# Attention and involution on one core: the last image's first convolution made directly, new cost constants, smaller last blocks, last units in parts

## The chip, the cores and the metric

The kernel runs on one core of a Trainium2 chip. The metric is the device time of one execution in microseconds (us). The core has five engines that run side by side and wait for each other by semaphores: TensorE (PE in the profile; its weight loads are PEld), VectorE (DVE), ScalarE (ACT), GpSimd (POOL) and SyncE (SP, which here only issues DMAs). All data is fp32. An fp32 matmul shows as two TensorE instructions in the trace.

## The reference

Input x has 4 images of 512 channels and 64 x 64 pixels (n = 4096). Two layers follow each other:

```
q, k, v = wq x + bq, wk x + bk, wv x + bv        # 512 -> 128 channels
x = wo (v softmax(q^T k)^T) + bo + x              # attention over the 4096 pixels
o = relu(s1 * (W1 x) + b1)                        # first convolution, 512 -> 128
w = Ws relu(sr * (Wr o) + br) + bs                # 8 groups x 49 taps for each pixel
y[c, p] = sum over 49 taps of w[group(c), tap, p] * o[c, p shifted by tap]
out = s3 * (W3 y) + b3 + x                        # 128 -> 512
```

The 7 x 7 neighbourhood is padded with zeros by 3 on each side. A group has 16 channels.

## The kernel before

**Chunks and images.** An image is cut into 8 chunks of 512 pixels (8 image rows). For each image, `keys_values` makes keys and values for all chunks (weights `wk`, `wv`), then `attention` goes through the chunks' queries. A step of attention is one 128 x 512 tile of scores: `pss` (TensorE), `pt` = exponential (ScalarE), `po` += values (TensorE), and `pacc` += `pt` on VectorE, which gathers the softmax denominators. A chunk has 32 steps. In the last image the last chunk is done as two blocks of 256 queries with 16 steps each. Scores are made two steps ahead. The `pss` and `pt` tiles have 2 and 5 buffers.

**Finishing a block** (`finish_block`, L520): `on` is copied from `po`, the denominators are summed (`sums`, `blocks`, `pl`), inverted (`rls`) and spread (`spread`), and `on` is multiplied by them. Four matmuls `pwo` with the output weights follow; L560 adds each to x, with the bias `bo`. The first convolution `p1` (four matmuls over the new x) and its Relu `o1` (L573) come next. In the last image `o1` is transposed by TensorE (`pp`) and written to a padded image in DRAM (`pix`). `pr` and `red` make the 32 reduced channels that the tap weights come from, and `last_bias` adds the last bias to x.

**Units.** The involution works in units of 4 image rows (two tiles of 2 rows, 128 pixels each; 16 units an image). Rows come back from `pix` into a ring of 12 rows, where entry r holds the 7 shifted copies of rows r and r+1. `pump` (L240) issues those loads as rows are written and ring space is free (`low`, `load`). For a unit, `weights` makes the tap weights `pw`. Then VectorE multiplies ring rows by weights (`prod`, or `acc` for the first, L356): for each of 7 column shifts once 4 row shifts (128 x 1024 elements) and once 3 (128 x 768). Where the ring wraps, a group is split in two. GpSimd adds each product to `acc` (L380). After attention of the last image has ended (`tail` is set), every second product is added by TensorE, as matmuls with the identity into `pa` (L375). At the end the parts of `acc` are folded (L389; in the tail by TensorE into `pa`), turned to channels first (`accT`), multiplied by W3 (`py`) and added to x (L461). Then the chunk, or in the last chunk the half, is stored.

**What sets the order.** The order is written by a planner while the program is built. Attention's steps run in a fixed loop. After each, `chores` (L269) takes one step of finishing, one of closing, and as many taps as `pace` allows. `pe` is the planner's TensorE clock; `free["dve"]` and `free["pool"]` are times at which it thinks that VectorE and GpSimd will have done what they were given, kept by the constants of L68 to L70. A tap is issued only if

```
pe >= max(begin, landed)
free["dve"] <= pe + 3.5          # 4.5 in the last image
free["pool"] <= pe + lag         # 4.0 during keys and values, 7.5 in attention
```

and if the budget `due` (1.56 tap rows a microsecond, at most 20) is at least 2. In the last image `pause` and `until` hold a finishing block until the planner thinks that VectorE is done with the step before. In the tail none of this holds: finishing, closing and taps take turns. Products have 4 buffers, tap weights 1 (2 in the tail), `red` has 3, and the general PSUM pool (`mm`) 2.

The kernel also holds a general path that runs only if a check of the denominators fails; it plays no part here.

Of the kernel before, what the change touches and what calls it, by code (L numbers as in the profile page):

```python
# [15 lines left out]
P = 128  # L16
# [42 lines left out]
SR = UR + K - 2  # L59

DYS = (0, 4), (4, 3)
TAPS_A_US = 1.56

PE_COLUMN = 0.43 / 256
DVE_OP, POOL_OP = 0.7, 1.28  # L68
DVE_TAPS, POOL_TAPS = (0.16, 0.27), (0.19, 0.55)
ROW_US, X_US, PIX_US, LAND_US = 2.2, 3.8, 1.5, 3.0  # L70
HOP_US = 0.8
STEP_US = 1.0
# [11 lines left out]
def fast_path(  # L84
# [91 lines left out]
    def takes(engine, us):  # L176
        free[engine] = max(free[engine], pe) + us
        return free[engine]
# [61 lines left out]
    def pump():  # L240

        nonlocal load
        while load // STEP in written:
            b, row = divmod(load, STEP)
            rows, us = written[b]

            end = H + SR - UR if rows == H else rows + PAD - 1
            n = min(b * STEP + end, low + RING) - load
            n = min(n, RING - load % RING, PIECE if b == B - 1 else RING)
            if n <= 0:  # L250
                break
# [20 lines left out]
        pace()  # L272


    def weights(b, u):
        red, col = reds[b, u]
        wpools.append(wpools.pop(0))
        pw = wpools[0].tile([P, NT, CH], F32, tag="w", name=f"pw_{b}_{u}")
        for t in range(NT):

            rows = slice(t * (P // NT), t * (P // NT) + CR + 1)
            pixels = slice(col, col + P)
            mm(
                pw[:, t, : NTAP * G], red[rows, pixels], wt[rows, O_WT : O_WT + NTAP * G],
                shared=2,
            )
        return pw
# [15 lines left out]
        nc.vector.tensor_scalar(verdict, pn, P - 0.5, None, ALU.is_lt)  # L303


    def involution():
        nonlocal low, due
        while True:
            while not units:
                yield "none"  # L310
            b, u = units.pop(0)
            acc = work2.tile([P, NT, 4, P], F32, tag="acc", name=f"acc_{b}_{u}")
            yield from until(free["dve"] + 0.3)
            pw = early.pop((b, u), None) or weights(b, u)
# [9 lines left out]
            for o, (x, dy, n) in enumerate(ops):  # L324
                if o and dy >= DYS[1][0] > ops[o - 1][1]:
                    low = base + UR
                    pump()
                    if tail and units:
                        early[units[0]] = weights(*units[0])
                rows = [(base + dy + t * 2) % RING for t in range(NT)]  # L330
                while base + dy + n + NT > load:
                    yield "wait"
                landed = max(landing[base + dy + i] for i in range(n + NT))
                while not tail and (
                    pe < max(begin, landed)
                    or free["dve"] > pe + (4.5 if b == B - 1 else 3.5)
                    or free["pool"] > pe + lag
                ):
# [4 lines left out]
                d0 = dy - DYS[dy >= DYS[1][0]][0]  # L343
                first = x == 0 and dy < DYS[1][0]
                prod, p0 = acc, d0
                if not first:
                    prod, p0 = prods.tile(
                        [P, NT, 4, P], F32, tag="prod", name=f"prod_{b}_{u}_{o}"
                    ), 0
                col = (x * K + dy) * G  # L350
                lines = ring[:, rows[0] : rows[0] + n, x, :]
                image = bass.AP(
                    tensor=lines.tensor, offset=lines.offset,
                    ap=[lines.ap[0], [(rows[1] - rows[0]) * K * P, NT], [K * P, n], [1, P]],
                )
                product = nc.vector.tensor_tensor(  # L356
                    prod[:, :, p0 : p0 + n, :].rearrange("p t d (g c) -> p t d g c", g=G),
                    image.rearrange("p t d (g c) -> p t d g c", g=G),
                    pw[:, :, col : col + n * G].unsqueeze(3)
                    .broadcast_to([P, NT, n * G, GC])  # L360
                    .rearrange("p t (d g) c -> p t d g c", d=n),
                    ALU.mult,
                )
                if not tail:
                    tc.keep_in_program_order(product)
                if first:
                    pass
                elif tail and o % 2:

                    begun = pa is not None  # L370
                    if not begun:
                        pa = ps1.tile([P, NT, P], F32, tag=("po", "acc")[u % 2], name=f"pa_{b}_{u}")
                    for t in range(NT):
                        for d in range(n):
                            mm(  # L375
                                pa[:, t, :], prod[:, t, d, :], ident,
                                not begun and t == d == 0, False,
                            )
                else:
                    nc.gpsimd.tensor_tensor(  # L380
                        acc[:, :, d0 : d0 + n, :], acc[:, :, d0 : d0 + n, :], prod[:, :, :n, :],
                        ALU.add,
                    )
                yield
            low = max(low, (b + 1) * STEP if u == NU - 1 else base + UR)
            pump()
# [133 lines left out]
    def finish_block(b, c, off, n, po, sums):  # L520

        late = b == B - 1
        name = f"{b}_{c}_{off}"
        xt = xs[b, c][:, :, off : off + n]

# [29 lines left out]
        yield from pause(takes("dve", DVE_OP * n / CH), 5)  # L555
        for t in range(CT):
            pw = ps.tile([P, CH], F32, tag="mm", name=f"pwo_{name}_{t}")[:, :n]
            mm(pw, w_slice(O_WO, t), on)
            takes("dve", DVE_OP * n / CH)
            nc.vector.scalar_tensor_tensor(  # L560
                xt[:, t, :], pw, bo[:, t : t + 1], xt[:, t, :], ALU.add, ALU.add
            )
            for _ in range(t % 2 if late else 1 + (t != 1)):
                yield
        for _ in range(0 if late else 2):
            yield
        p1 = ps.tile([P, CH], F32, tag="mm", name=f"p1_{name}")[:, :n]
        for t in range(CT):
            mm(p1, w_slice(O_W1, t), xt[:, t, :], t == 0, t == CT - 1)
            if t == 1 and not late:  # L570
                yield
        o1 = work1.tile([P, CH], F32, tag="o1", name=f"o1_{name}")[:, :n]
        nc.scalar.activation(o1, p1, AF.Relu, bias=v1(V_B1), scale=v1(V_S1))  # L573

        def last_bias():

# [41 lines left out]
                    )  # L618
        us = takes("dma", PIX_US) + LAND_US

        pr = ps.tile([P, CH // NT], F32, tag="mm", name=f"pr_{name}")[:, : n // NT]
        for t in range(NT):
            half = slice(t * (P // NT), (t + 1) * (P // NT))
            mm(
                pr[half], w_slice(O_WP, 0)[:, half],
                o1.rearrange("p (u t x) -> p u t x", t=NT, x=P)[:, :, t, :], shared=2,
            )
        red = redpool.tile([P, CH // NT], F32, tag="red", name=f"red_{name}")[:, : n // NT]
        nc.scalar.activation(red, pr, AF.Relu, bias=v1(V_BP), scale=v1(V_SP))
        for i in range(tiles // NT):  # L630
            reds[b, top // UR + i] = red, i * P

        rows = top + n // W
        written[b] = rows, us
        units.extend((b, u) for u in range(top // UR, rows // UR))
        pump()
        yield
        if late:
            yield from last_bias()
        if (b, c) == (B - 1, NCH - 3):  # L640
# [65 lines left out]
    for b in range(B):  # L706
# [3 lines left out]
        if b == 0:  # L710
# [3 lines left out]
                tc.keep_in_program_order(mm(pb[:, t : t + 1], w_slice(O_WO, t), v1(V_BVC)))  # L714
            bo = const.tile([P, CT], F32, name="bo")
            nc.vector.tensor_tensor(bo, pb, vec[:, V_BO : V_BO + CT], ALU.add)
        attention(b, *kv)
    tail.append(True)
    scorepool.close()
# [405 lines left out]
```

## Time and profile before

| | us |
|---|---|
| median of 3 runs | 2606.61 |
| lowest, highest | 2604.79, 2607.39 |
| span of the profiled execution | 2605.7 |
| TensorE busy | 2587.9 (99%) |
| VectorE busy | 1874.2 (72%) |
| GpSimd busy | 1823.5 (70%) |
| ScalarE busy | 835.8 (32%) |

The profiled execution's own time is known by its span, from the first to the last instruction; it lies among the timed runs. A group's line gives source line, engine, operation, tiles, shape, count, then busy time and the mean of one. A window's line gives busy time and instruction count of each engine, TensorE's granted clock, and the share and rate of DMA. A piece of the chain is start, duration and what ran.

Units can be told apart in the trace by their first product, which writes `acc`. In the last image they start at 2070, 2103, 2150, 2189, 2223, 2262, 2295, 2333, 2368, 2408, 2439, 2478, 2514, 2542, 2556 and 2578 us. The blocks' reductions (`red`) are at 2047, 2115, 2192, 2265, 2336, 2408, 2477, 2516 and 2542 us, and the last `sums` of attention is at 2523.4.

### The profile page before, as it was taken

Reading aid. Unit: us, or ns where it says so; the run is one execution under the profiler, and the core shown is the slowest. Engines: PE = TensorE matmul, PEld = TensorE weight load, DVE = VectorE, ACT = ScalarE, POOL = GpSimd, SP = SyncE. Lnnn points to the kernel's source line nnn. Section 1 sums busy time; section 2 is a strip of 40 time slices with the busy share of each in tenths; the row PEclk is TensorE's granted clock in tenths of the full one; section 3 lists DMA queues with packets and bytes.
Section 4 is the critical chain, followed back from the end, with each engine's and each line's share of the span. In section 5 each row is a group of like instructions: output and inputs, shape, how many; then the busy total and the mean of one; then the engine's idle time right before and its main releaser. Section 6 shows DMA issues by size and latency. Waiting matters only on the chain.

```text
span 2605.7 us, 24569 instructions
## 1 busy us (share of the span) xinstructions
PE 2587.9 (99%) x7484; PEld 1246.5 (48%) x7484; DVE 1874.2 (72%) x2677; ACT 835.8 (32%) x1378; POOL 1823.5 (70%) x1197
## 2 busy tenths in 40 slices
PE   9999999999999999999999999999999999999998
PEld 7444444445544444444644444444464444444577
DVE  0447777877575787788676678788757678777887
ACT  1333333332233333333223333333323333333330
POOL 0007788877881788887885468888788577877886
PEclk9999999999999999999999999999999999999999
DMA  6033232445615344233651434443463433222343
GB/s 236 1 75 63 55 85 73 99 99 150 164 43 112 63 101 95 61 84 82 180 129 45 103 69 101 101 92 74 118 171 83 101 93 93 72 60 58 73 91 102
DMA packets 208798, 244.33 MB, mean 94 GB/s; under 512 B 109640, under 2 KB 128528, under 8 KB 208528
## 3 DMA queue, kind: packets, MB, share of 16 engines
q1 hardware_dynamic: 208224, 242.31, 38.6%
q8 instruction: 61, 1.00, 0.2%
q14 instruction: 81, 0.66, 0.1%
q10 hardware_dynamic: 432, 0.36, 0.0%
HBM read 193.57 MB, written 49.06 MB: 93 GB/s over the span
## 4 chain that ended last, share of the span: by engine, by line
PE 91%; POOL 4%; DVE 3%; issue 1%; DMA 0%; ACT 0%; SPq 0%; POOLq 0%; DVEq 0%; ACTq 0%
PE pss L220 32%; PE po L220 31%; PE pv L220 4%; PE pk L220 4%; PE pq L220 4%; PE pwo L220 4%; PE py L220 4%; PE p L220 4%; POOL acc L380 4%; PE pw L220 2%; DVE prod L356 1%; PE pa L220 1%; DVE pacc L696 1%; PE pr L220 1%; POOL acc L389 0%
## 5 line engine op out<-in xcount | busy, mean ns | idle before, releaser
L380 POOL TENSOR_TENSOR acc<-acc,prod 128x768 f32<-128x768 f32 (+3 forms) x1063 | 1701.5, 1620 | 760.5 <-DVE prod L356 712.4
L220 PE MATMUL pss<-q,k 128*128 128x512 f32 (+1 forms) x2112 | 1056.3, 585 | 0.0
L220 PE MATMUL po<-pt,v 128*128 128x512 f32 (+1 forms) x2112 | 1047.7, 581 | 0.0
L665 ACT ACTIVATE pt<-pss 128x512 f32<-128x512 f32 x1024 | 611.3, 597 | 1252.0 <-PE pss L220 1184.9
L356 DVE TENSOR_TENSOR prod<-ring,pw 128x512 f32<-128x512 f32 (+3 forms) x1092 | 886.7, 847 | 44.6 <-POOL acc L380 41.7
L696 DVE TENSOR_TENSOR pacc<-pacc,pt 128x512 f32<-128x512 f32 x958 | 664.6, 694 | 243.2 <-ACT pt L665 216.2
L220 PEld LDWEIGHTS po<-pt,v 128*128 128x128 f32 x2112 | 399.3, 190 | 482.2 <-issue 462.2
L220 PEld LDWEIGHTS pss<-q,k 128*128 128x128 f32 x2112 | 391.9, 190 | 466.2 <-issue 459.3
L404 DVE STREAM_TRANSPOSE turned<-acc 128x256 f32<-128x256 f32 x48 | 21.4, 446 | 217.4 <-POOL acc L389 217.4
L220 PE MATMUL py<-accT,wt 128*128 128x512 f32 (+1 forms) x264 | 132.3, 584 | 4.0 <-DVE x L461 3.3
L220 PE MATMUL pwo<-on,wt 128*128 128x512 f32 (+1 forms) x264 | 130.3, 586 | 0.0
L220 PEld LDWEIGHTS pv<-wt,x 128*128 128x128 f32 x1024 | 119.6, 192 | 15.3 <-issue 15.0
L389 POOL TENSOR_TENSOR acc<-acc 128x512 f32<-128x512 f32 x120 | 119.5, 996 | 9.4
L461 DVE SCALAR_TENSOR_TENSOR x<-py,vec,x 128x512 f32<-128x512 f32 (+1 forms) x132 | 95.7, 726 | 36.1 <-PE py L220 35.8
L220 PE MATMUL pv<-wt,x 128*128 128x128 f32 x1024 | 120.2, 275 | 0.0
L220 PE MATMUL p<-x,wt 128*128 128x512 f32 (+1 forms) x264 | 119.2, 579 | 0.0
L578 ACT ACTIVATE x<-x,vec 128x512 f32<-128x512 f32 (+1 forms) x132 | 92.9, 706 | 80.0 <-PE p L220 74.9
L220 PE MATMUL pk<-x,wt 128*128 128x512 f32 x256 | 117.3, 596 | 0.1
L220 PE MATMUL pq<-x,wt 128*128 128x512 f32 (+1 forms) x264 | 115.4, 580 | 0.0
L560 DVE SCALAR_TENSOR_TENSOR x<-pwo,bo,x 128x512 f32<-128x512 f32 (+1 forms) x132 | 95.2, 727 | 22.8 <-PE pwo L220 21.7
L356 DVE TENSOR_TENSOR acc<-ring,pw 128x1024 f32<-128x1024 f32 (+1 forms) x84 | 78.7, 955 | 17.6 <-PE pw L220 17.6
L220 PEld LDWEIGHTS pq<-x,wt 128*128 128x128 f32 x264 | 50.0, 190 | 60.2 <-issue 56.7
(57 smaller groups left out, 733.6 us busy)
## 6 DMA issues: line engine op xcount, KB each, us to landing
x<-x_dram SPq DMA_DIRECT2D x55, 1024.0 KB, 5.7
ring<-pix SPq DMA_DIRECT2D x74, 448.0 KB, 8.3
ring<-pix SPq DMA_DIRECT2D x24, 1344.0 KB, 9.7
out_dram<-x SPq DMA_DIRECT2D x31, 1024.0 KB, 4.2
ring<-pix SPq DMA_DIRECT2D x24, 896.0 KB, 10.7
ring<-pix SPq DMA_DIRECT2D x30, 672.0 KB, 10.2
ring<-pix SPq DMA_DIRECT2D x6, 2240.0 KB, 19.5
pix<-o1t SPq DMA_DIRECT2D x192, 32.0 KB, 1.7
```

What stands on the lines that cost most here:

```text
L220: return nc.tensor.matmul(o, lhsT=lhsT, rhs=rhs, start=start, stop=stop)
L356: product = nc.vector.tensor_tensor(prod[:, :, p0 : p0 + n, :].rearrange("p t d (g c) -> p t d g c", g=G), image.rearrange("p t d (g c) -> ...
L380: nc.gpsimd.tensor_tensor(acc[:, :, d0 : d0 + n, :], acc[:, :, d0 : d0 + n, :], prod[:, :, :n, :], ALU.add,)
L389: nc.gpsimd.tensor_tensor(acc[:, :, :n, :], acc[:, :, :n, :], acc[:, :, n : 2 * n, :], ALU.add)
L404: nc.vector.transpose(blocks.rearrange("p (t k q) -> p t k q", t=NT, q=TB), acc[:, :, 0, :].rearrange("p t (k q) -> p t k q", q=TB),)
L461: nc.vector.scalar_tensor_tensor(xt[:, t, :], py, v1(V_S3 + t), xt[:, t, :], ALU.mult, ALU.add)
L560: nc.vector.scalar_tensor_tensor(xt[:, t, :], pw, bo[:, t : t + 1], xt[:, t, :], ALU.add, ALU.add)
L578: nc.scalar.activation(xt[:, t, :], xt[:, t, :], AF.Identity, bias=v1(V_B3 + t))
L665: nc.scalar.activation(pt, pss, AF.Exp)
L696: nc.vector.tensor_tensor(paccs[k], paccs[k], pt, ALU.add)
```

## The change

Four things change together.

1. **Direct first convolution** for chunks 5 to 7 of the last image. Between keys and attention of the last image the product of output weights and first convolution is made (`w1wo`, with its bias `b1wo`). In these blocks `p1` is four matmuls over the old x plus one, `w1wo` on `on`. The residual (`pwo` and L560) comes after `o1` has been written and reduced.
2. **Constants** of the account: VectorE and GpSimd operations and taps are charged less.
3. **The last chunk's queries** in blocks of 256, 128 and 128. A block of 128 has one tile, so reductions are kept by tile (`reds`).
4. **Units 14 and 15 of the last image** are done in nine parts, given by tiles, first row shift and number of row shifts. Row shifts that meet only padding are left out, two ring rows are not loaded, and the part's number and column shift decide which engine adds.

The body of a tap becomes the function `multiply_add`.

```diff
+PADDED = 2
+LAST = (
+    (0, (0, 1), 0, 2), (0, (0, 1), 2, 2),
+    (0, (0, 1), 4, 2), (0, (0,), 6, 1), (1, (0,), 0, 4),
+    (0, (1,), 6, 1), (1, (1,), 0, 4), (1, (0, 1), 4, 1), (1, (0,), 5, 2),
+)
+DIRECT = 5
-DVE_OP, POOL_OP = 0.7, 1.28
-DVE_TAPS, POOL_TAPS = (0.16, 0.27), (0.19, 0.55)
+DVE_OP, POOL_OP = 0.62, 1.23
+DVE_TAPS, POOL_TAPS = (0.065, 0.267), (0.14, 0.545)
...
-            end = H + SR - UR if rows == H else rows + PAD - 1
+            end = H + SR - UR - PADDED * (b == B - 1) if rows == H else rows + PAD - 1
...
-    def weights(b, u):
-        red, col = reds[b, u]
-        wpools.append(wpools.pop(0))
-        pw = wpools[0].tile([P, NT, CH], F32, tag="w", name=f"pw_{b}_{u}")
-        for t in range(NT):
+    def weights(b, u, tiles=range(NT), pw=None):
+        if pw is None:
+            wpools.append(wpools.pop(0))
+            pw = wpools[0].tile([P, NT, CH], F32, tag="w", name=f"pw_{b}_{u}")
+        for t in tiles:
+            red, col = reds[b, u * NT + t]
...
+    def last_units(b, u0):
+        nonlocal low, due
+        accs, pas, pws, weighed = {}, {}, {}, set()
...
+        for i, (v, tiles, dy, n) in enumerate(LAST):
+            u = u0 + v
+            while v and not tail:
+                yield "wait"
+            base = b * STEP + u * UR
+            while base + dy + 2 * tiles[-1] + n > load:
+                yield "wait"
...
+            fresh = [t for t in tiles if (v, t) not in weighed]
+            if fresh:
+                pws[v] = weights(b, u, fresh, pws[v])
+                weighed.update((v, t) for t in fresh)
...
+            for x in range(K):
...
+                pas[v] = multiply_add(
+                    b, u, accs[v], pas[v], pws[v], tiles, x, dy, n, f"{i}_{x}",
+                    x == 0 and dy < DYS[1][0], bool(tail) and (x + i) % 2,
+                )
+                yield
+            if ends[v] == i:
+                closing.append(turn_unit(b, u, accs[v], pas[v], takes("pool", POOL_OP * 1.5)))
+        units.clear()
...
     def involution():
...
             b, u = units.pop(0)
+            if b == B - 1 and u == NU - 2:
+                yield from last_units(b, u)
+                return
...
     def finish_block(b, c, off, n, po, sums):
+        direct = late and c >= DIRECT
...
+        spreads = takes("dve", DVE_OP * n / CH)
+        def residual():
...
+        if not direct:
+            yield from pause(spreads, 5)
+            yield from residual()
...
+            mm(p1, w_slice(O_W1, t), xt[:, t, :], t == 0, t == CT - 1 and not direct)
+        if direct:
+            yield from pause(spreads, 0)
+            mm(p1, w1wo, on, False, True)
+        nc.scalar.activation(
+            o1, p1, AF.Relu, bias=b1wo if direct else v1(V_B1), scale=v1(V_S1)
+        )
...
+        if direct:
+            yield from residual()
         if late:
             yield from last_bias()
...
     def attention(b, kt, vT, q):
-            blocks[-1:] = [(NCH - 1, off, CH // 2) for off in (0, CH // 2)]
+            blocks[-1:] = [(NCH - 1, 0, 2 * P), (NCH - 1, 2 * P, P), (NCH - 1, 3 * P, P)]
...
+        if b == B - 1:
+            turned = work1.tile([P, CT, P], F32, tag="sums", name="wo_turned")
+            pt = ps.tile([P, CT, P], F32, tag="mm", name="pwot")
+            for t in range(CT):
+                nc.tensor.transpose(pt[:, t, :], w_slice(O_WO, t), ident)
+            nc.vector.tensor_copy(turned, pt)
+            pc = ps.tile([P, P + 1], F32, tag="mm", name="pc")
+            for t in range(CT):
+                mm(pc[:, P:], w_slice(O_W1, t), bo[:, t : t + 1], t == 0, t == CT - 1)
+            for t in range(CT):
+                mm(pc[:, :P], turned[:, t, :], w_slice(O_W1, t), t == 0, t == CT - 1)
+            w1wo = const.tile([P, P], F32, name="w1wo")
+            b1wo = const.tile([P, 1], F32, name="b1wo")
+            nc.scalar.copy(w1wo, pc[:, :P])
+            nc.vector.scalar_tensor_tensor(
+                b1wo, pc[:, P:], v1(V_S1), v1(V_B1), ALU.mult, ALU.add
+            )
         attention(b, *kv)
```

More of the change, by code (lines that the diff above doesn't have):

```diff
@@ L303, in tell, with multiply_add @@
         nc.vector.tensor_scalar(verdict, pn, P - 0.5, None, ALU.is_lt)
+    def multiply_add(b, u, acc, pa, pw, tiles, x, dy, n, o, first, by_pe):
+        base = b * STEP + u * UR
+        ts = slice(tiles[0], tiles[-1] + 1)
+        nt = len(tiles)
+        rows = [(base + dy + t * 2) % RING for t in tiles]
+        d0 = dy - DYS[dy >= DYS[1][0]][0]
+        prod, p0 = acc, d0
+        if not first:
+            prod, p0 = prods.tile([P, NT, 4, P], F32, tag="prod", name=f"prod_{b}_{u}_{o}"), 0
+        col = (x * K + dy) * G
+        lines = ring[:, rows[0] : rows[0] + n, x, :]
+        image = bass.AP(
+            tensor=lines.tensor, offset=lines.offset,
+            ap=[lines.ap[0], [(rows[-1] - rows[0]) * K * P, nt], [K * P, n], [1, P]],
+        )
+        product = nc.vector.tensor_tensor(
+            prod[:, ts, p0 : p0 + n, :].rearrange("p t d (g c) -> p t d g c", g=G),
+            image.rearrange("p t d (g c) -> p t d g c", g=G),
+            pw[:, ts, col : col + n * G].unsqueeze(3)
+            .broadcast_to([P, nt, n * G, GC])
+            .rearrange("p t (d g) c -> p t d g c", d=n),
+            ALU.mult,
+        )
+        if not tail:
+            tc.keep_in_program_order(product)
+        if first:
+            pass
+        elif by_pe:
+            begun = pa is not None
+            if not begun:
+                pa = ps1.tile([P, NT, P], F32, tag=("po", "acc")[u % 2], name=f"pa_{b}_{u}")
+            for t in tiles:
+                for d in range(n):
+                    mm(
+                        pa[:, t, :], prod[:, t, d, :], ident,
+                        not begun and t == tiles[0] and d == 0, False,
+                    )
+        else:
+            nc.gpsimd.tensor_tensor(
+                acc[:, ts, d0 : d0 + n, :], acc[:, ts, d0 : d0 + n, :], prod[:, ts, :n, :],
+                ALU.add,
+            )
+        return pa
@@ L342, in involution @@
                 due -= n
-                d0 = dy - DYS[dy >= DYS[1][0]][0]
                 first = x == 0 and dy < DYS[1][0]
[L345 to L383, printed above, removed]
+                by_pe = bool(tail) and o % 2
+                pa = multiply_add(b, u, acc, pa, pw, (0, 1), x, dy, n, o, first, by_pe)
                 yield
@@ L619, in finish_block @@
         us = takes("dma", PIX_US) + LAND_US
-        pr = ps.tile([P, CH // NT], F32, tag="mm", name=f"pr_{name}")[:, : n // NT]
-        for t in range(NT):
+        pr = ps.tile([P, CH // NT], F32, tag="mm", name=f"pr_{name}")[:, : max(n // NT, P)]
+        first = top // 2
+        whole = tiles > 1
+        for t in range(NT) if whole else [first % NT]:
             half = slice(t * (P // NT), (t + 1) * (P // NT))
[L624 to L631, printed above, removed]
+            pixels = o1
+            if whole:
+                pixels = o1.rearrange("p (u t x) -> p u t x", t=NT, x=P)[:, :, t, :]
+            mm(pr[half], w_slice(O_WP, 0)[:, half], pixels, shared=2 if whole else 1)
+        red = redpool.tile([P, CH // NT], F32, tag="red", name=f"red_{name}")[:, : max(n // NT, P)]
+        filled = slice(0, P) if whole else half
+        nc.scalar.activation(
+            red[filled], pr[filled], AF.Relu,
+            bias=v1(V_BP)[filled], scale=v1(V_SP)[filled],
+        )
+        for i in range(tiles):
+            reds[b, first + i] = red, i // NT * P
         rows = top + n // W
```

45 lines of the change are left out of this document (32 added, 13 removed).

## The prediction, made before the changed kernel was built

> **What bounds the kernel now.** I read the page first, then the chain, then the tail by stages, and last the groups of the stretch that feeds the tail.
>
> The page's busy line and its clock slices:
>
> ```profile
> PE 2587.9 (99%) x7484; PEld 1246.5 (48%) x7484; DVE 1874.2 (72%) x2677; ACT 835.8 (32%) x1378; POOL 1823.5 (70%) x1197
> PEclk9999999999999999999999999999999999999999
> ```
>
> TensorE is full from the first slice to the last. So there are two ways to change the time: TensorE instructions before attention ends, which count one for one, and the tail after the last exponential, when only taps, the last block's finish and the closing are left. The chain at that seam and at the very end:
>
> ```profile
> 2506.91 0.86 PE pss L220 x4
> 2507.77 0.86 PE po L220 x4
> ...
> 2522.82 0.61 ACT pt L665
> 2523.45 0.70 DVE sums L699
> ...
> 2531.59 1.19 PE pa L220 x4
> 2532.79 1.71 PE pwo L220 x4
> ```
>
> Before 2523 the chain is scores and outputs without a gap: four 256-column instructions in 0.86, 0.215 us each. After it the chain changes hands between VectorE, TensorE and GpSimd. From 2523.4 to the end of the span (2605.7) is a tail of 82.3 us. Its five stages (rest of unit 12 with the last block's finish; unit 13; 14; 15; the end), split at the accumulator-starting products:
>
> ```profile
> core 0: us, PE busy (x) PEld busy (x) DVE busy (x) ACT busy (x) POOL busy (x), PEclk, DMA share, GB/s
> 2523.40:2541.50 18.10, 14.78 (x64) 11.43 (x62) 15.28 (x23) 2.34 (x7) 14.51 (x8) 0.81 0.25 56
> 2541.50:2556.30 14.80, 14.78 (x118) 13.06 (x119) 12.88 (x20) 1.54 (x4) 9.28 (x6) 1.00 0.79 192
> 2556.30:2577.50 21.20, 20.02 (x136) 16.18 (x136) 20.18 (x32) 0.37 (x1) 15.70 (x13) 1.00 0.45 119
> 2577.50:2593.30 15.80, 14.30 (x116) 13.21 (x115) 15.04 (x18) 0.37 (x1) 13.64 (x8) 1.00 0.08 26
> 2593.30:2605.70 12.40, 5.72 (x36) 4.47 (x36) 2.69 (x6) 0.37 (x1) 1.06 (x1) 0.85 0.22 72
> ```
>
> TensorE and VectorE are both about full, so the tail is a matter of how much work is left over, not of rows that are late. Before it, units 8 to 12 each in its own window:
>
> ```profile
> 2366.00:2411.00 45.00, 45.00 (x117) 19.65 (x116) 38.02 (x56) 16.50 (x28) 32.12 (x25) 1.00 0.09 30
> 2411.00:2440.90 29.90, 29.90 (x78) 13.88 (x77) 24.08 (x30) 10.40 (x18) 28.80 (x15) 1.00 0.59 123
> 2440.90:2477.60 36.70, 36.70 (x133) 23.17 (x132) 30.04 (x47) 13.92 (x23) 29.36 (x23) 1.00 0.08 29
> 2477.60:2513.90 36.30, 36.30 (x171) 31.28 (x172) 28.90 (x47) 13.58 (x25) 29.93 (x22) 1.00 0.52 109
> 2513.90:2523.40 9.50, 9.50 (x48) 8.06 (x49) 8.31 (x9) 4.22 (x9) 6.89 (x3) 1.00 0.43 101
> ```
>
> Here GpSimd, which adds every product, is the slow hand (28 to 31 us a unit), yet it idles 12.9, 1.1, 7.3 and 6.4 us in the first four windows. Those 27.7 us are all that earlier rows and another account can win.
>
> The profiled span, 2605.7, lies inside the timed runs (2604.79 to 2607.39) and 0.9 under their median, so I add nothing around it.
>
> **Part 1: merged weights and direct convolution.** *Setup*, once, between keys and attention of image 3, where TensorE is full. 4 transposes at 0.15 (4.3 us for 28 at L590), 8 one-column instructions at about 0.12 (0.5 for 4 of `pl`) and 8 of 128 columns at 0.117 (120.2 for 1024 of `pv`): 2.5 us. Between them stands a VectorE copy (0.67, the row of `pacc<-pt`). VectorE was idle for 6.06 us at that spot (until 1957.34), so the one-column instructions nearly cover it: 0.2. With one product (1.13) and a full backlog (3.5 by the planner's own limit) ahead of it, up to 4. Taken: 2.7. The ScalarE copy and the small VectorE operation behind it have nobody waiting for 60 us.
> *The extra matmul* `w1wo` on `on`: two instructions of 0.43 for 512 columns. Chunks 5 and 6 and the 256 block: 0.86 + 0.86 + 0.43 = 2.15 us.
> *Latency.* In chunk 6 the multiply of `on` starts at 2457.1 and the first-convolution Relu at 2474.0. Between them stand a planner's pause, four `pwo` with two yields, four residual additions and `p1`. After the change only the pause, one matmul and the Relu are left: about 10 us less. Those rows gate unit 11's second half (first product 2493.25; reduction 2477 plus the planner's 14 for the first three ring rows is 2491); chunk 5 gates unit 9's in the same way. The `pwo`, residual and bias steps move behind the pixel DMAs; SP issues the same DMAs in the same order, two ring rows fewer at the end.
>
> **Part 2: account.** The new constants price a 4-row product at 1.13 and a `pacc` addition at 0.62. The trace's own start-to-start times are 1.14 and 0.60 to 0.65; the old prices, 1.24 and 0.70, kept VectorE emptier than planned. For GpSimd the new 2.32 is under the row's 2.36, but each unit is charged for first products that GpSimd never adds, so a unit is charged 30.5 to 31.5 and takes about 30. VectorE in the windows of units 8, 10 and 11 is 80 to 84% busy. If it went to 95% each would shorten by about 5 us, 15 together. Bounds for how much earlier unit 12 starts against TensorE's work: 0 (a landing takes over) and 27.7. I take 10: the windows still hold the chunk finishes, and each unit change costs GpSimd 2 to 4 us.
>
> **Part 3: blocks 256, 128, 128.** Scores and outputs of the last 256 queries were 128 instructions of 0.215 (27.5) and become 256 of 0.117 (30.0): 2.4 us. The bounds are 0.107 (half of 0.215), at which it costs nothing, and 0.122, the tail's `pa<-ident,prod`, at which it costs 3.7. The `pv` row is nearest, since it too changes weights at every 128 columns. A second small `pq`, `pwo`, `p1` and the denominators (`pl`, four matmuls a block in place of two): 0.9 before the end.
> The Trainium skill, "TensorE: Matmul & The Clock Gate", section "Back-to-back issue gap", speaks against this part: sustained pairs of weight load and matmul take about 81 ns at 128 columns and 131 at 512, so a column in a narrow matmul costs 2.5 times a wide one's. By that ratio part 3 would cost some 40 us and the kernel would come to about 2645, an estimate from that page. The trace's 0.117 against 0.43 for four times the columns is a ratio of 1.09, and I go by it.
>
> **Part 4: last units in parts.** Unit 14 was 14 products of 512 elements and 7 of 768, unit 15 7 of 1024 and 7 of 768: at 0.61, 0.88 and 1.14 that is 28.8 us. Now it is 35 of 512, 14 of 256 (0.345) and 14 of 128. No row shows the last; half of the 256 row is 0.17, the row itself 0.345, and the straight line through the other rows gives 0.21. The sum is 29.1 (28.5 to 30.9). So the skipped zero rows pay for the smaller instructions and nothing more. TensorE adds 82 tile-rows in place of 90, at 0.244: 2.0 less. But unit 13 still asks ahead for unit 14's weights, nobody takes them, and they are made again (0.9), in the buffer that unit 13's last product reads. VectorE then waits for TensorE once: 1.3 (0, if residual work fills it, to 2). Unit 15's weights come tile by tile (0.4). VectorE +1.6, TensorE -0.7: I take +0.8. At the end one small GpSimd addition (0.73) precedes the 16 `pa` instructions, where 28 took 3.41: -0.6.
> That rows come earlier (62 after the first 128 block) is worth nothing here: the ring loads of the tail were issued from 2545 to 2552, and the products that need them began at 2570.
>
> **The sum.** Added to TensorE before attention ends: 2.7 + 2.15 + 2.4 + 0.9 = 8.1, of which 3.7 fall after unit 12 has begun. Unit 12's lead over the end of attention grows from 9.5 to 9.5 + 10 + 3.7 = 23.2 us. Less 2.5 until GpSimd's first addition, 20.7 hold six 4-row additions (2.42 with the gap) and three 3-row ones (1.88), and VectorE is one ahead: about 2.7 products of 0.88 are left, 2.4 us, where now two of 1.14 and seven of 0.88 are, 8.4. Saved: 6.0. Two of chunk 5's `py` additions (0.66) move ahead: 1.3. The shorter finish returns 1.0 of the 2.8 that VectorE idles in the first stage; the second block's residual takes 0.6. Gain: 7.7. From 2605.7: +8.1 - 7.7 + 0.8 - 0.6 = 2606.3, so 2606.
>
> **Rivals.** *Unit 13 begins before attention ends* (faster). GpSimd's idle is nearly all recovered: 20 us earlier leaves nothing of unit 12 and takes all four `py` along: 2601; the whole 27.7 gives 2597. For it: 27.7 us of idle and rows 10 us earlier. Against: VectorE is at 80% already, and the second block's finish falls into the same stretch. It decides from 20 us on.
> *The added TensorE work is not paid back* (slower). Unit 12 comes no earlier, because VectorE's finish work or a landing sets the pace as now; only the 3.7 us help. Saved are 1.8 of taps and 1.0 of idle, less 0.6: 2605.7 + 8.1 - 2.2 + 0.2 = 2612, over the bound where the gain in start is under about 1 us.
> *TensorE stalls by the account* (slower). With honest prices VectorE really runs 3.5 to 4.5 us behind, and the five exponential buffers leave, by my estimate from steps of 1.72 us, about 2 us before TensorE waits. Now the trace shows no wait of `pss` or `po` for VectorE. Half a microsecond in each of 33 blocks is 16 us: 2622; a tenth of that is 2608.
>
> **How the numbers follow.** My forecast, no change, 45; unit 13 early 30, of which a part stays near 2601; not paid back 14; stalls 11. 0.2% is 5.2 us, about what a measurement of this kernel can tell. Range: 2596 (below the fast case, for a tail that packs better than the rows say) to 2615 (past the unpaid case, with a little stalling). Faster 0.30, same 0.45, slower 0.25. The forecast's own range is 2602 to 2611.
>
> **What would show it.** Right: `sums` of the last block about 8 us later than 2523.4; the setup a TensorE piece of 2.5 to 3 at 1955; 128-column `pss` and `po` at 0.117; the Relu of chunk 6 about 7 us after its `on` multiply; unit 12's first product 20 us or more before the last `sums`; units 14 and 15 within 1 us of 37. Wrong: waits of `pss` or `po` for VectorE in images 0 to 2 (account); unit 12's lead under 15 (not paid) or over 33 (fast case); 128-wide products at 0.3 or more.

## The result: slower by 1.15%

The changed kernel takes 2636.8 us (median of 4 runs, 2630.7 to 2642.5) against 2606.6: a ratio of 1.0115, 95% interval 1.0103 to 1.0128. I had forecast 2606 with 2596 to 2615. Its runs also spread over 12 us, where those of before spread over 3.

The page of the changed kernel, its busy line and the clock slices:

```profile
PE 2599.9 (99%) x7564; PEld 1248.3 (47%) x7564; DVE 1884.1 (71%) x2715; ACT 838.1 (32%) x1388; POOL 1838.3 (70%) x1218
PEclk9999999999999999999999999999999999999999
```

Nothing looks wrong here: TensorE is still at 99%, and the slices hide what a stretch of a few microseconds does. The last `sums` of each part place the loss. Images 0 to 2 end at 1882.1 before and 1908.7 after, although nothing but the cost constants differs there: +26.6. Image 3 takes 641.4 and 665.9 until attention ends: +24.6. The tail takes 82.2 and 62.7: -19.5. Together that is +31.7, as the span grew (2605.7 to 2637.3).

The waits of TensorE in images 0 to 2 (60 to 1880 us), before and after (who waited for whom: sum, times, longest):

```profile
PE py L220 <- DVE x L461: 3.3, 3, 1.1
PE pw L220 <- DVE prod L356: 0.7, 3, 0.2
```
```profile
PE pw L229 <- DVE prod L331: 12.2, 5, 2.6
PE py L229 <- DVE x L525: 3.8, 3, 1.5
PE pq L229 <- DVE x L525: 3.2, 2, 2.4
```

4.0 us have become 19.2. TensorE waits for VectorE to read out a PSUM buffer that TensorE wants to write: the tap weights `pw`, one buffer before the tail, and the general pool of two (`py`, `pq`). One such place in TensorE's order of time, changed kernel:

```profile
372.99 1.02 PE L229 MATMUL po<-pt,v 128*128 128x512 f32 x2
376.55 1.68 PE L229 MATMUL pw<-wt,red 33*128 33x392 f32 x4 [2.54 <-DVE prod L331]
378.16 2.07 PE L229 MATMUL pss<-q,k 128*128 128x512 f32 x2
```

After 2.54 us of idling the scores take 2.07 where they take 1.02 otherwise. The window there and the next show why (granted clock is the number before the last two):

```profile
376.20:383.00 6.80, 6.45 (x10) 2.72 (x11) 3.04 (x6) 0.60 (x1) 4.94 (x6) 0.50 0.25 38
383.00:390.00 7.00, 7.00 (x19) 2.78 (x18) 6.61 (x12) 2.36 (x4) 3.95 (x4) 1.00 0.72 140
```

The clock falls to half for 6.8 us. In images 0 to 2 such stretches sum to 23.9 us, before to 3.4; half of the difference, 10.2, is lost. With the 15.2 us of longer waits that is about 25.4 of the 26.6.

And why VectorE was late there, from its own order of time just before:

```profile
363.02 0.69 DVE L331 TENSOR_TENSOR prod<-ring,pw 128x512 f32<-128x512 f32 x1 [1.30 <-POOL acc L355]
365.45 0.42 DVE L331 TENSOR_TENSOR prod<-ring,pw 128x256 f32<-128x256 f32 x1 [1.14 <-POOL acc L355]
366.80 0.69 DVE L331 TENSOR_TENSOR prod<-ring,pw 128x512 f32<-128x512 f32 x1 [0.93 <-POOL acc L355]
...
371.66 2.30 DVE L780 TENSOR_TENSOR pacc<-pacc,pt 128x512 f32<-128x512 f32 x3
373.87 0.70 DVE L680 STREAM_TRANSPOSE o1t<-o 128x512 f32<-128x512 f32 x1
374.49 1.91 DVE L331 TENSOR_TENSOR prod<-ring,pw 128x512 f32<-128x512 f32 x4
```

Here VectorE stood waiting for GpSimd to free a product buffer, with `pacc` additions queued behind the product. Three of them then run in a row, a transpose follows, and the products that still read the old `pw` end only at 376.4, when TensorE goes on. This is one place; whether the same holds for the whole loss is taken up below.

### The profile page after: what moved, and what is told of

Read it like the earlier page. It is cut to its first block, busy times and chain, and to the rows that moved or that the text cites. A ratio compares the mean times of both kernels' runs of the same rounds, so it can differ in the third digit from the quotient of the medians.

```text
span 2637.3 us, 24792 instructions
## 1 busy us (share of the span) xinstructions
PE 2599.9 (99%) x7564; PEld 1248.3 (47%) x7564; DVE 1884.1 (71%) x2715; ACT 838.1 (32%) x1388; POOL 1838.3 (70%) x1218
## 4 chain that ended last, share of the span: by engine, by line
PE 80%; POOL 9%; issue 5%; DVE 5%; DMA 1%; ACT 0%; SPq 0%; POOLq 0%; DVEq 0%; ACTq 0%
PE pss L229 29%; PE po L229 28%; POOL acc L355 7%; PE pq L229 4%; PE p L229 4%; PE pwo L229 4%; PE py L229 3%; PE pk L229 3%; PE pv L229 3%; DVE prod L331 2%; DVE pacc L780 2%; PE pw L229 2%; POOL acc L453 1%; PE pa L229 1%; PE pr L229 1%
## 5 line engine op out<-in xcount | busy, mean ns | idle before, releaser
L355 POOL TENSOR_TENSOR acc<-acc,prod 128x768 f32<-128x768 f32 (+4 forms) x1082 | 1714.2, 1604 | 777.2 <-DVE prod L331 732.4
L229 PE MATMUL pss<-q,k 128*128 128x512 f32 (+2 forms) x2176 | 1061.3, 574 | 0.0
L229 PE MATMUL po<-pt,v 128*128 128x512 f32 (+2 forms) x2176 | 1050.8, 570 | 0.0
L331 DVE TENSOR_TENSOR prod<-ring,pw 128x512 f32<-128x512 f32 (+4 forms) x1119 | 892.0, 831 | 77.0 <-POOL acc L355 59.8
L229 PEld LDWEIGHTS pss<-q,k 128*128 128x128 f32 x2176 | 397.3, 191 | 468.5 <-issue 460.5
L229 PE MATMUL pwo<-on,wt 128*128 128x512 f32 (+2 forms) x272 | 130.7, 573 | 1.9 <-DVE x L627 1.9
L229 PEld LDWEIGHTS pv<-wt,x 128*128 128x128 f32 x1024 | 120.1, 192 | 18.1 <-issue 17.7
L229 PE MATMUL pq<-x,wt 128*128 128x512 f32 (+2 forms) x272 | 119.3, 582 | 5.6 <-DVE x L525 5.6
L229 PE MATMUL p<-x,wt 128*128 128x512 f32 (+2 forms) x272 | 120.4, 572 | 0.0
L654 ACT ACTIVATE x<-x,vec 128x512 f32<-128x512 f32 (+2 forms) x136 | 94.0, 694 | 74.2 <-PE p L229 58.2
L627 DVE SCALAR_TENSOR_TENSOR x<-pwo,bo,x 128x512 f32<-128x512 f32 (+2 forms) x136 | 96.0, 713 | 21.9 <-PE pwo L229 20.8
L229 PEld LDWEIGHTS pq<-x,wt 128*128 128x128 f32 x272 | 51.0, 194 | 66.9 <-issue 54.8
## 6 DMA issues: line engine op xcount, KB each, us to landing
ring<-pix SPq DMA_DIRECT2D x6, 2240.0 KB, 19.5
```

The costliest lines, as they stand in the source:

```text
L229: return nc.tensor.matmul(o, lhsT=lhsT, rhs=rhs, start=start, stop=stop)
L331: product = nc.vector.tensor_tensor(prod[:, ts, p0 : p0 + n, :].rearrange("p t d (g c) -> p t d g c", g=G), image.rearrange("p t d (g c) - ...
L355: nc.gpsimd.tensor_tensor(acc[:, ts, d0 : d0 + n, :], acc[:, ts, d0 : d0 + n, :], prod[:, ts, :n, :], ALU.add,)
L627: nc.vector.scalar_tensor_tensor(xt[:, t, :], pw, bo[:, t : t + 1], xt[:, t, :], ALU.add, ALU.add)
L654: nc.scalar.activation(xt[:, t, :], xt[:, t, :], AF.Identity, bias=v1(V_B3 + t))
```

## The experiments

Ratios are each run's own against runs of the kernel before on the same chip, with 95% intervals.

**The account: is it what costs?** e1 is the changed kernel with the old constants:

```diff
-DVE_OP, POOL_OP = 0.62, 1.23
-DVE_TAPS, POOL_TAPS = (0.065, 0.267), (0.14, 0.545)
+DVE_OP, POOL_OP = 0.7, 1.28
+DVE_TAPS, POOL_TAPS = (0.16, 0.27), (0.19, 0.55)
```

> The changed kernel with all four cost constants of before; direct convolution, 256/128/128 blocks and parts stay. Theory A (the account makes VectorE late, TensorE waits for PSUM that VectorE has to free, and the clock falls to half after each wait): images 0 to 2 are the program of before, so the last sums of image 2 are back at 1882 us (1909 in the changed kernel), no pw or pq wait over 1.2 us, at most one half-clock stretch before the tail; the whole is 2606.6 + 8.1 added TensorE work - 4 to 12 in the tail: 2603 to 2611. Rival B (the direct convolution, blocks and parts cost the time): stays at 2625 or more.

2614.2 us (1.0027, 1.0016 to 1.0039): 22.6 under the changed kernel. Image 2 ends at 1880.9, TensorE's waits are back at 4.0, and no half-clock stretch is left before the tail. Image 3 takes 653.1 until attention ends, so of its +24.6 some 11.7 come with the other three parts and 12.9 with the account. The total is 3 over the expected band, which is the business of the second half below.

e2 is the kernel before with the new constants alone (the same edit the other way).

> The kernel before with the new constants alone. Theory A: images 0 to 2 lose 25 to 29 us as in the changed kernel (last sums of image 2 at about 1909), image 3 loses 5 to 10 more until attention ends, the tail gives back 5 to 15: 2620 to 2640. Rival B: within 5 us of before, 2602 to 2612.

2637.1 us (1.0122, 1.0105 to 1.0139), image 2 ends at 1903.9. So the account alone costs 30 us, theory A holds and B falls. Inside the whole change it costs 22.6, and the other three parts cost 7 (e1): the two do not simply add up. The split was less well foreseen: by its trace images 0 to 2 lose 21.8 (25 to 29 expected), image 3 loses 15.9 (5 to 10), and the tail gives back 11.3.

**Which price?** e3 restores only GpSimd's (`POOL_OP` 1.28, `POOL_TAPS` (0.19, 0.55)), e4 only VectorE's (`DVE_OP` 0.7, `DVE_TAPS` (0.16, 0.27)) in the changed kernel.

> The changed kernel with GpSimd's constants of before and VectorE's new ones. If VectorE's backlog against TensorE (its own price) makes it late: 2620 or more, waits of pw and pq as in the changed kernel. If GpSimd's price does (VectorE waits for product buffers: 59.8 us in the changed kernel, 41.7 before): 2603 to 2613, and VectorE's wait for GpSimd back to about 42 us.

> The changed kernel with VectorE's constants of before and GpSimd's new ones. The mirror of the last: if GpSimd's price makes VectorE late, 2620 or more and VectorE's wait for GpSimd near 60 us; if VectorE's own price does, 2603 to 2613. If each does a part, both this and the last lie between 2610 and 2630.

2619.2 (1.0049, 1.0032 to 1.0066) and 2619.9 (1.0049, same interval). Neither mirror image came, but the third case did, in which each does a part: either new price alone costs 5 to 6 us over e1, both together 22.6. VectorE's waits for GpSimd before a product did go to opposite sides over the span: 43.3 us in e3 and 68.9 in e4, where the changed kernel has 59.8. So the old prices of VectorE take as much of the loss away without shortening these waits.

**Does asking later help?** In e9, the kernel before with the new account, a unit's weights wait for VectorE's planned end and 3.0 us more:

```diff
-            yield from until(free["dve"] + 0.3)
+            yield from until(free["dve"] + 3.0)
```

> The kernel before with the new account (2637.1 alone), but a unit's tap weights are asked for when the planner's VectorE has been free for 3.0 us, not 0.3. If TensorE's loss comes from asking VectorE for a PSUM buffer that it has not read out yet, the waits of pw go (12.0 us in images 0 to 2, five of them, and with them the half-clock stretches that follow each): last sums of image 2 at 1885 to 1893 in place of 1904, the whole 2612 to 2625; waits of py, pq and pwo stay. If VectorE's lateness costs by itself, whatever asks first, the loss only moves to the scores: 1900 or later, 2630 or more.

2635.5 (1.0107, 1.009 to 1.0124), image 2 ends at 1911. My theory of the single `pw` buffer falls. The waits of `pw` went, but turned up elsewhere (60 to 1880 us of e9):

```profile
PE py L220 <- DVE x L461: 12.6, 6, 3.8
PE pl L220 <- DVE blocks L537: 4.6, 2, 2.3
PE pwo L220 <- DVE x L560: 3.8, 7, 1.3
PE pw L220 <- DVE prod L356: 1.3, 3, 0.5
```

Whatever TensorE asks of VectorE next meets its lateness. I then measured that lateness itself: for every exponential of images 0 to 2, the time from its end on ScalarE to the start of its addition to `pacc` on VectorE, matched in order (768 in every trace). The last two columns are VectorE's waits for GpSimd before a product, 60 to 1880 us, and the last `sums` of image 2.

| kernel | median us | 90% under | 99% under | waits for GpSimd | image 2 ends |
|---|---|---|---|---|---|
| before | 2.6 | 5.5 | 8.3 | 31.7 | 1882.1 |
| changed | 2.8 | 7.4 | 9.8 | 43.0 | 1908.7 |
| e1, old account | 2.7 | 5.5 | 8.4 | 31.9 | 1880.9 |
| e2, account alone | 2.8 | 7.4 | 9.8 | 45.2 | 1903.9 |
| e3, GpSimd's old price | 2.5 | 5.3 | 7.9 | 28.1 | 1890.0 |
| e4, VectorE's old price | 2.2 | 5.6 | 7.9 | 48.2 | 1889.3 |
| e9, weights asked later | 2.9 | 6.8 | 9.9 | 43.2 | 1910.8 |
| e14, VectorE's limit tight | 1.5 | 6.2 | 8.5 | 40.9 | 1921.8 |
| e15, GpSimd's lag tight | 2.1 | 5.0 | 6.8 | 24.3 | 1887.3 |

From before to changed the median hardly moves; the late tenth does. The runs e14 and e15 are explained next.

**Whose lateness?** Both in the kernel before with the new account. e14 tightens VectorE's limit, e15 GpSimd's:

```diff
e14
-                    or free["dve"] > pe + (4.5 if b == B - 1 else 3.5)
+                    or free["dve"] > pe + (3.0 if b == B - 1 else 2.0)
e15
-POOL_LAG = 4.0, 7.5
+POOL_LAG = 4.0, 5.5
```

> The kernel before with the new account (2637.1), and the planner may put VectorE 2.0 us ahead (3.0 in the last image) in place of 3.5 (4.5). If the loss is VectorE's lateness, for which the old prices were a hidden reserve: the wait from an exponential's end to its addition falls from a 90th percentile of 7.4 us to 6.0 or less (before: 5.5), and the time to 2605 to 2615. If it is GpSimd's lateness that reaches VectorE through the product buffers: 2622 or more.

> The kernel before with the new account, VectorE's limits as they were, GpSimd's lag in attention 5.5 in place of 7.5. The mirror: if GpSimd's lateness is the cause, 2605 to 2615 and VectorE's wait for product buffers (45 us in images 0 to 2, 32 before) under 35; if VectorE's own, 2622 or more. If it takes both, both this and the last lie between 2615 and 2625.

e14: 2652.0 (1.0177, 1.016 to 1.0194), worse than the account with the old limit. e15: 2612.6 (1.0023, 1.0012 to 1.0035), 24 of the 30 us back. VectorE's waits for a product buffer, 60 to 1880 us, before, e2 (the account with the old limits), e14 and e15:

```profile
DVE prod L356 <- POOL acc L380: 31.7, 50, 1.8
```
```profile
DVE prod L356 <- POOL acc L380: 45.2, 86, 1.3
```
```profile
DVE prod L356 <- POOL acc L380: 40.9, 65, 1.7
```
```profile
DVE prod L356 <- POOL acc L380: 24.3, 45, 1.1
```

So with the new prices, of these two limits it is GpSimd's lag that has to be held back; a lag of 7.5 goes with prices that were too high. Why a tight limit for VectorE makes it worse than the old one I did not find out: its waits for GpSimd stay near those of e2 and `py` waits rise from 3.8 to 9.8, so I take it that taps come bunched, but that is argued, not shown.

That VectorE's waits for GpSimd are the path by which the prices reach TensorE is not shown either, since their sum does not follow the time. e4 has the most of them (48.2), and its image 2 ends 7 us late; e14 has less than the changed kernel, and ends 40 late. What does follow the time is TensorE's side of it: in e2, e9 and e14 TensorE's longer waits for VectorE and half of the added half-clock time make about 20 of 22, 25 of 29 and 37 of 40 us up to the end of image 2.

e17 puts the same 5.5 into the whole change.

> The whole change with GpSimd's lag in attention 5.5 in place of 7.5, all else as changed (2636.8). If GpSimd's lateness is what the account costs here too: last sums of image 2 at 1884 to 1889 (1909), 2611 to 2619, that is the 2614.2 of the old account within 5. If the direct path, blocks or parts need the old account for another reason: 2622 or more.

2617.1 (1.0038, 1.0024 to 1.0052): 19.7 under the changed kernel, image 2 ends at 1889.5. The same limit takes most of the loss away there.

**The other three parts, with the old account.** Together (e1) they cost 7 us. Each was left out in turn: e5 sends units 14 and 15 through the old path and loads all rows (`PADDED = 0`), e6 puts the last chunk back to 256 and 256, e7 sets `DIRECT = NCH` and leaves the merged weights out, and e8 keeps only the direct convolution (the edits of e5 and e6 together).

> Old account, direct convolution and 256/128/128 blocks, units 14 and 15 as before (no parts, all ring rows loaded). Old account with all three is at 2614.2. Theory P (prediction's terms: parts are worth 0, blocks cost 3.3): 2612 to 2616. Theory Q (parts cost time: unit 14's weights are made twice, the small products bind on hand-overs): 2607 to 2611.

> Old account, direct convolution and parts, last chunk in 256/256 as before. Theory P: 3.3 us of TensorE work go, 1.6 us of lead go with them: 2611 to 2614. If the two small blocks cost what the time of the last sums says (40.0 us for the last 256 queries against 33.6): 2607 to 2610.

> Old account, 256/128/128 blocks and parts, no direct convolution and no merged weights. Theory P: 4.9 us of added work go, and unit 12's earlier start goes too (about 5 us): 2612 to 2616. If the direct path is worth more than it costs, 2617 or more; if it is a loss, 2611 or less.

> The kernel before with the direct convolution alone (old account, 256/256, units as before). Theory P: +2.7 setup, +2.15 matmuls, tail shorter by 4 to 6: 2605 to 2608. If blocks and parts are what costs (Q): 2598 to 2604, faster than before. If the direct path itself is the loss: 2610 or more.

| kernel | us | ratio (95%) |
|---|---|---|
| e1, all three | 2614.2 | 1.0027 (1.0016 to 1.0039) |
| e5, direct + blocks | 2607.8 | 1.0006 (0.9997 to 1.0015) |
| e6, direct + parts | 2605.6 | 1.0000 (0.9990 to 1.0009) |
| e7, blocks + parts | 2612.0 | 1.0022 (1.0013 to 1.0032) |
| e8, direct alone | 2600.6 | 0.9982 (0.9973 to 0.9991) |

The direct convolution is the one part that wins: 0.18% alone, and faster than both kernels. By the medians parts cost 5 to 6 us (e8 to e6, e5 to e1), the small blocks 7 to 9 (e8 to e5, e6 to e1). Theory Q holds in e5 and e8, e7 lies on the lower edge of theory P's band, and e6 is faster than either of its bands. Where direct convolution wins, in the window of the tail's first 18 us and in that of units 10 and 11; before, then e8 (the same two windows by the clock):

```profile
2439.00:2513.90 74.90, 74.90 (x307) 55.33 (x308) 60.85 (x95) 28.09 (x49) 61.11 (x45) 1.00 0.29 67
2523.40:2541.50 18.10, 14.78 (x64) 11.43 (x62) 15.28 (x23) 2.34 (x7) 14.51 (x8) 0.81 0.25 56
```
```profile
2439.00:2513.90 74.90, 74.90 (x305) 53.73 (x304) 61.89 (x95) 27.64 (x50) 66.93 (x48) 1.00 0.31 73
2523.40:2541.50 18.10, 17.61 (x90) 13.21 (x89) 17.45 (x25) 3.56 (x7) 17.17 (x11) 1.00 0.25 78
```

GpSimd works 66.9 us in place of 61.1 in the first, since rows come earlier. In the second, where e8's attention runs on for 6.8 us, TensorE hardly idles at the seam any more (0.5 us, 3.3 before), and its clock stays at 1.00 where it fell to 0.81.

**What of the parts costs?** Both runs change e6. e10 cuts the nine parts to the old products (rows of padding still left out); e11 keeps the nine and lets unit 14 take the weights that unit 13 asked for:

```diff
e10
-LAST = (
...
-)
+LAST = (
+    (0, (0, 1), 0, 2), (0, (0, 1), 2, 2), (0, (0, 1), 4, 3),
+    (1, (0, 1), 0, 4), (1, (0, 1), 4, 1), (1, (0,), 5, 2),
+)
e11
-                pas[v], pws[v] = None, None
+                pas[v], pws[v] = None, early.pop((b, u), None)
+                weighed.update((v, t) for t in tiles if pws[v])
```

> Direct convolution, 256/256, old account (2600.6 with units as before, 2605.6 with nine parts); the last two units go through the parts' function, but in six parts that are the products of before (unit 14: 2, 2, 3 row shifts of both tiles; unit 15: 4, then 1 of both and 2 of one tile). If the 28 small products (256 and 128 elements) cost the 5 us: 2600 to 2602. If what surrounds them does (unit 14's weights made twice, in the buffer that unit 13 still reads): 2604 to 2606.

> Direct convolution, 256/256, old account and the nine parts (2605.6), but unit 14 takes the weights that unit 13 has asked for ahead. The mirror of the last: if the second making costs the 5 us, 2600 to 2602; if the small products do, 2604 to 2606; prediction's price for it is 1.3 to 2.2.

2603.0 (0.9985, 0.9975 to 0.9994) and 2604.3 (0.9990, 0.9980 to 1.0000). Neither alone is the whole, and the stages tell them apart. Unit 13's stage and the rest up to the end, of e6, e10 and e11:

```profile
2532.90:2554.40 21.50, 21.01 (x149) 17.62 (x147) 18.33 (x33) 3.58 (x8) 16.49 (x14) 1.00 0.65 155
2554.40:2603.60 49.20, 37.63 (x240) 30.36 (x238) 35.68 (x75) 1.12 (x3) 28.03 (x29) 0.94 0.13 45
```
```profile
2533.60:2555.10 21.50, 21.01 (x148) 17.60 (x146) 18.61 (x33) 3.58 (x8) 16.76 (x14) 1.00 0.65 160
2555.10:2601.60 46.50, 34.58 (x236) 28.66 (x234) 33.62 (x54) 1.12 (x3) 27.02 (x20) 0.96 0.14 48
```
```profile
2533.20:2552.00 18.80, 18.39 (x134) 16.36 (x135) 18.13 (x33) 3.59 (x8) 15.62 (x13) 1.00 0.64 154
2552.00:2601.50 49.50, 38.10 (x248) 30.13 (x246) 35.56 (x75) 1.12 (x3) 28.81 (x30) 0.96 0.17 52
```

The second making of weights costs 2.7 us in unit 13's stage (21.5 against 18.8). Nine parts in place of six cost about 2.7 after it (49.2 to 49.5 against 46.5). That e10 also changes the order of the two units' products and makes unit 15's weights at once leaves open whether the small products themselves cost this. In e8 the two stages take 18.8 and 46.8.

**Tuning what wins.** e13 is e8 with the new account in the last image alone; e16 and e18 start the direct convolution at chunk 6 and chunk 4; e19 is e8 with a lag of 6.5.

```diff
e13
     for b in range(B):
+        if b == B - 1:
+            globals().update(
+                DVE_OP=0.62, POOL_OP=1.23, DVE_TAPS=(0.065, 0.267), POOL_TAPS=(0.14, 0.545)
+            )
e16
-DIRECT = 5
+DIRECT = 6
e18
-DIRECT = 5
+DIRECT = 4
e19
-POOL_LAG = 4.0, 7.5
+POOL_LAG = 4.0, 6.5
```

> The kernel before with the direct convolution (2600.6), and the new account in the last image alone. Images 0 to 2 as before (last sums of image 2 at 1881). If an honest account brings unit 12 forward as the prediction had it and the waits it makes in one image stay under that: 2592 to 2599. If the waits of one image (a third of 27 us, so about 9) outweigh it: 2602 to 2612.

> The direct convolution alone, old account, from chunk 6 on (2600.6 from chunk 5 on). Chunk 5's extra matmul (0.86) goes; if unit 10 is brought forward by unit 9's second half only through chunk 5, unit 12 comes up to 4 us later and the tail grows by up to 2: 2599.5 to 2602.

> The direct convolution alone, old account, from chunk 4 on (2600.6 from 5 on, 2605.5 from 6 on). One more extra matmul costs 0.86. If chunk 4's rows hold unit 7's second half as chunk 5's hold unit 9's, unit 12 comes 2 to 8 us earlier: 2596 to 2600. If units 8 to 11 are by then bound by GpSimd and VectorE: 2600.5 to 2603.

> The direct convolution alone from chunk 5 on, old account, GpSimd's lag 6.5 in place of 7.5. The old prices show 4.0 us of TensorE waits before the last sums (six); a shorter lag can take away at most these, and slows GpSimd before the tail: 2599 to 2606, no gain beyond 2.

e13: 2607.3 (1.0002, 0.9992 to 1.0011). The account loses 6.7 us even where its backlog could help the tail; attention of image 3 shows a wait of `pwo` of 3.6 us and one of `pq` of 2.45. e16: 2605.5 (0.9998, 0.9989 to 1.0008), a miss: chunk 5 is worth 5 us. With it unit 12 starts 25.5 us before the last `sums` (e8), without it 19.9 (e16). e18: 2601.4 (0.9982, 0.9972 to 0.9991), the same as e8: unit 12's lead stays at 25.5. e19: 2608.5 (1.0007, 0.9997 to 1.0017), outside my band and 8 over e8. By the traces 2.7 us of that fall into images 0 to 2, 1.4 into image 3 and 4.0 into the tail. VectorE's waits for GpSimd (60 to 1880 us) rise here from 31.8 to 40.7, where the same kind of step lowered them in e15. So a shorter lag helps only together with the new prices; why it hurts with the old ones is not shown. e8 is the best that I ran.

## Why the prediction was wrong

**The failing step is part 2, the account.** I costed it as a gain of 10 us of lead in image 3 and put its cost at nothing, there and in images 0 to 2. Alone it costs 30 us (e2), inside the change 22.6 (e1). Two sentences were wrong. "each unit is charged for first products that GpSimd never adds, so a unit is charged 30.5 to 31.5 and takes about 30" is an average over a unit; at 363 to 371 us GpSimd fell behind by enough to hold VectorE's products up, and e15 and e17 show that less room for this takes most of the loss away. How much of the whole loss goes by this path stays open (e4, e14). And the prices were read as honest or dishonest, when the old ones were a reserve that went with the limit of 7.5.

**The third rival was the right mechanism at 11 in 100, with the wrong place and price.** I looked for waits of `pss` and `po` behind the five exponential buffers; they came at `pw`, `py`, `pq` and `pwo`, whose PSUM buffers are fewer. I did not count the clock: for each added microsecond of waiting in images 0 to 2 about 0.7 more was lost at half clock. 16 us stood for it, 30 was measured alone.

**The fast rival's mechanism came true as well.** Unit 13 began 12.0 us before the last `sums`, and unit 12's lead was 47.6 us, over the 33 that I named. The tail shrank by 19.5. But the account's share of the lead was bought for the most part by TensorE's delay. In e2 the lead grew from 9.6 to 24.3, while attention of image 3 took 15.9 us longer; in e13 it is 15.3 more than in e8, and 10.6 of these are the later end of attention.

**Part 1.** The setup: the image boundary is 139.6 before and 141.7 with it, 2.1 against 2.7. The latency: 16.9 us from `on` to Relu in chunk 6 became 3.6 in e8, 13 against "about 10". The gain was too low: in e8 unit 12's lead is 25.5 (I had 23.2, with the account's 10 and the small blocks' time in it) and unit 13 starts 2.9 after the last `sums` in place of 18.1, 15.2 against my 7.7; unit 13's stage then took 18.8 in place of 14.7, since the last block's finish fell into it.

**Part 3.** The price was too high for the matmuls: e1's chain has

```profile
2515.43 0.89 PE pss L229 x8
2516.32 0.89 PE po L229 x8
```

0.111 us for 128 columns, so 256 of them cost 0.9 more and not 2.4. By the figures of the Trainium skill's "Back-to-back issue gap" ("TensorE: Matmul & The Clock Gate"), 81 ns at 128 columns and 131 at 512, a narrow column would be 2.5 times as dear; here it is 1.03 times (0.111 against a quarter of 0.43), and the measurement decides. Yet the two blocks cost 7 to 9 us, where I had 3.3 less some lead. By spans e5 is 4.6 over e8, 3.3 of it before the last `sums`; the traced execution of e5 took 2605.1, 2.6 under its median, and so shows only that much. What makes the rest I can't place.

**Part 4.** Sized +0.8, measured 5 to 6. The second making of the weights was foreseen at 1.3 on VectorE and 0.9 on TensorE and is 2.7. The products' own times were foreseen rightly: in e11's tail they start 0.60, 0.33 and 0.20 us apart at 512, 256 and 128 elements, against 0.61, 0.345 and 0.21. What my sum left out lies between the engines: in the stages after unit 13 VectorE waits 1.7 us for GpSimd in e6, 0.6 in e10 and 0.4 in e8. That is a part of the other 2.7; the rest is open. Whether earlier rows are worth anything in the tail no run here separates.

## What to carry to other kernels

A planner's prices and its limits are one setting: a price that is corrected to the truth can take away a reserve that a limit was tuned with, and the limit has to move with it (e2 and e15); moved alone it costs as well (e19). A stage that an average calls balanced can still be late within each group; look at the late tenth of the waits beside the mean. Where one engine is full, ask of every buffer that it fills who empties it: here `pw`, with one buffer, had 12.2 of the 19.2 us of waits.

## What the runs showed of the hardware

TensorE's clock fell to half at short waits or just after them: at one of 2.54 us (for 6.8 us) in the changed kernel, and in e4 at two of three waits of 1.84 us (for 3.4 us each). Waits of 1.1 us, which come at three places in images 0 to 2 before, in e1 and in e8, left it whole at eight of the nine. But two waits of 2.8 us in e15 and one of 2.25 in the changed kernel left it whole too, so the length of a wait alone does not decide; what else does is open. All half-clock stretches before the last `sums` are 3.4 or 6.8 us long. The Trainium skill ("TensorE: Matmul & The Clock Gate", section "What's actually happening") has the clock halve after an idle window of some 3.4 us that runs freely; the length of the stretches agrees, but here less than a whole window of idling was enough (1.84 us). The 12 us of spread of the changed kernel's runs go along with a mean granted clock of 0.992 to 0.996: the slowest run has the lowest.
